# Two attention blocks on one core: a weight's sums and the weight loads behind the softmax sums' trips, a variance product one step earlier, the last block in two halves

## The chip, the core and the metric

The kernel runs on one core of one Trainium2 chip. The core has five engines that run side by side and meet through semaphores: TensorE (PE, the matrix products), VectorE (DVE), ScalarE (ACT), GpSimd (POOL), and SyncE (SP), which here issues nearly all DMA transfers. [...]The metric is device time in microseconds (us), the median of several executions; everything is float32.

## The reference, cut to what matters

Eight images of 512 channels by 1024 positions go through two attention blocks. Written for one image x (512 x 1024):

```
# block 0: 8 heads of 64 channels
h = group_norm(x, 32 groups);  q, k, v = Wqkv @ h + b
w = softmax(q_head^T k_head / sqrt(64));  a_head = v_head w^T
x = x + Wp @ a + bp
# block 1: one head of 512 channels
h = group_norm(x, 8 groups);  q, k, v = Wq @ h, Wk @ h, Wv @ h   (+ biases)
w = softmax(q^T k / sqrt(512))
x = x + Wp @ (v w^T) + bp
```

## The kernel before

**Products of weights.** Block 1 is rewritten: q^T k becomes h^T (Wq^T Wk) h and Wp Wv becomes one matrix. So the prologue computes two 512 x 512 products of weights, called m and z (`product`, L838). Each is copied out of PSUM by ACT (L848), stored to DRAM (L850), and loaded again in quarters (`prepare`, L279).

**Strassen's scheme in Winograd's form.** Nearly every large product is made of seven products of quarters instead of eight. `wino` (L229) does one such product: `step(p)` runs product p for two row blocks i, in three pairs of PSUM banks a, b and c, and `done` is called when an output quarter (row, column) is complete; u2 (the tile u) and u3 (the tile w) are partial results that DVE adds up at products 6 and 7 (`upper`, L240). The last two products, 4 and 3, are put on a list (`tail`) and run inside the next stage, by `finish`. Hooks are functions called after each step, and `background` is a list from which every step takes a few functions more (`back`). The factors need sums of quarters: four additions or subtractions of 128 x 512 on DVE for a weight (`left_sums`, called in `prepare`, L289 and L290). For the two-level form of the products (`conv2`), `keep2` (L300) makes four more on DVE or POOL, and SP stores seven pieces (L316). `keep` (L294) stores the one-level factors of a weight, 1.8 MB (L295); `load_weight` (L327) loads the factors of the next use, 1.3 or 1.8 MB (L335, L338).

**The prologue** (L871) handles the first image and all weights: transposes of Wk and Wq, the product m with the group norm's two small products inside it as hooks (`group_mean` after product 6, `affine` after product 9, counting from 0), then v (`by_token`), q and k of image 0, then the product z. `affine` (L121) is a small PE product over the groups, then one DVE instruction, four on POOL (L126 to L132), and then the scaling of the four tiles of the image, two on POOL and two on ACT. The background in v's stage holds the eight sums for the image's factors, and then the four sums for q and the four for k.

**Attention of block 0** (`attention0`, L639). The loop runs over four pairs of heads (hp) and two halves of the positions (tb). For each, PE makes eight score tiles (sc), ACT takes the exponential of each (e, L658), DVE adds the eight up (L660 and six times L662), and PE multiplies them with v (av). After tb = 1 the sums of the pair go on a trip (`reciprocals`, L593): PE adds over the partitions (sums), DVE copies the result out of PSUM (L617), SP stores it (L619) and loads it in another layout (L622), DVE takes reciprocals (L624), SP stores them (L625) and loads them twice as a broadcast (L635); a DVE or POOL multiplication then scales a (L696). The list `extra` has two slots for each (hp, tb): the even one is emptied between the scores and av, the odd one after av and before the trip. For image 0 these slots also hold what the prologue returns as `later`:

```
later = {
    1: steps, 2: [lambda: keep("z", t), load, load], 5: [load],
    12: [
```

Slot 1 is after the first av, slot 2 in the middle of the second block (hp 0, tb 1), slot 5 after av of hp 1, tb 0. `steps` are the four DVE sums for z, `load` a `load_weight`. What is pinned (`tc.keep_in_program_order`) keeps its place in the order of the program; what is not, may be moved on its engine by the scheduler.

**Attention of block 1** works on the image before the one in block 0; for the last image its `values1` (L790) is the end of the kernel. There a `wino` over the exponentials and z's factors makes the output quarters in the order of products 1, 2, 5, 6, 7, 4, 3. `done` adds the partial result u (L802), multiplies by the reciprocals r (L803), adds bias and residual (L805), and stores 128 x 512 numbers (L806). At the very end PE makes one 1 x 1 product (ps_good) for a flag that says whether all reciprocals were in range (L1213 to L1219), and every engine reads that flag (L1358) to decide on a slower general path, which isn't taken.

Of the kernel before, what the change touches and what calls it, by code (L numbers as in the profile page):

```python
# [12 lines left out]
ALU = mybir.AluOpType  # L13
AX = mybir.AxisListType

P = 128
# [13 lines left out]
def two_attention_blocks_kernel(  # L30
# [8 lines left out]
    nc = tc.nc  # L39
    B, C, T = x.shape  # L40
    KC = C // P
    HT = T // 2
# [16 lines left out]
    def matmul(*args, **kw):  # L59
        tc.keep_in_program_order(nc.tensor.matmul(*args, **kw))  # L60
# [113 lines left out]
    def main_path(ctx):  # L174
# [18 lines left out]
        def acc_tile(name):  # L193
            return ps_acc.tile([P, HT], F32, tag="acc", name=name)
# [14 lines left out]
        def load_x(b, c, what):  # L209
            t = big_tile(f"{what}_{b}_{c}")  # L210
            nc.sync.dma_start(t, x[b, c * P : (c + 1) * P, :])
            return t


        background = []
# [10 lines left out]
            while tail:  # L226
                tail.pop(0)()

        def wino(uid, mm, done, middle=(6, 2, 5, 7), hooks=(), after=(), back=2):  # L229

            hooks = list(hooks)
            ps, t1, u2, u3 = {}, {}, {}, {}
            bank = {1: "a", 2: "a", 6: "b", 7: "b", 4: "b", 5: "c", 3: "c"}

            def u_tile(what, i):
                return upool.tile([P, HT], F32, tag=f"{what}{i}", bufs=2 if what == "t" else 1, name=f"{what}{i}_{uid}")

            def upper(t, i, what):
                t[i] = u_tile(what, i)
                nc.vector.tensor_add(t[i], ps["b", i], t1[i])  # L240

            def step(p):
                n = bank[p]
                for i in range(2):
                    start = (n, i) not in ps
                    if start:
                        ps[n, i] = ps_pools["abc".index(n)].tile([P, HT], F32, tag="ps", name=f"ps{n}{i}_{uid}")
                    mm(p, i, ps[n, i], start)
                    if p == 1:
                        t1[i] = u_tile("t", i)  # L250
                        nc.scalar.copy(t1[i], ps["a", i])
                    elif p == 2:
                        done(i, 0, 0, ps["a", i], None)
                    elif p == 6:
                        upper(u2, i, "u")
                    elif p == 7:
                        upper(u3, i, "w")
                        done(i, 1, 1, ps["c", i], u3[i])
                    elif p == 4:
                        done(i, 1, 0, ps["b", i], t1[i])  # L260
                    elif p == 3:
                        done(i, 0, 1, ps["c", i], u2[i])
                run_background(back)
                for f in hooks.pop(0) if hooks else ():
                    f()

            step(1)
            finish()
            for p in middle:
                step(p)  # L270
            tail.extend([lambda: step(4), lambda: step(3), *after])


# [18 lines left out]
            return t, steps  # L292

        def keep(n, t):  # L294
            nc.sync.dma_start(wdram[n], t)  # L295


        wdram2 = {n: dram.tile([P, 7, 7, P], F32, name=f"sums2_{n}") for n in "qkmvp"}
# [489 lines left out]
            return total, {p: [x[:, i, :] for x in fs[p] for i in range(2)] for p in fs}  # L788

        def values1(b, zf, ef, r, xt, uid, hooks):  # L790
            def mm(p, i, ps, start):
                for k in range(4):
                    matmul(
                        ps, zf[p][k // 2][:, k % 2, ts(i, P)], ef[p][k], start=start and k == 0, stop=k == 3, skip_group_check=True
                    )

            def done(i, row, c, ps, u):
                oc = 2 * row + i

                o = acc_tile(f"o_{uid}_{oc}_{c}") if (row, c) == (1, 1) else ps  # L800
                if u is not None:
                    nc.vector.tensor_add(o, ps, u)  # L802
                nc.vector.tensor_mul(o, o, r[:, c, :])  # L803
                xh = xt[oc][:, ts(c, HT)]
                nc.vector.scalar_tensor_tensor(xh, o, obias[1][:, oc : oc + 1], xh, ALU.add, ALU.add)  # L805
                nc.sync.dma_start(out[b, oc * P : (oc + 1) * P, ts(c, HT)], xh)  # L806

            wino(f"av_{uid}", mm, done, middle=(2, 5, 6, 7), hooks=hooks, back=4)


        def raw(n, i):
# [59 lines left out]
        def prologue():  # L871
# [13 lines left out]
            def normed():  # L885
# [2 lines left out]
                    norm.apply(nc.scalar if c % 2 else nc.gpsimd, h0[c], h0[c], c)  # L888

            product(  # L890
                wq, wk, "m", {6: lambda: norm.group_mean(acc_tile("gmean_0_0")[:, :KC]), 9: normed},
            )
            raw_v = raw("v", 6)
            raw_p = raw("p", 7)
            for f in first["v"][1]:
                f()
            background.extend(steps)
            for n in "qk":
                background.extend(first[n][1])
            v = by_token(weight_factors(first["v"][0]), hf, "v0_0", middle=(2, 5, 6, 7), back=4)  # L900
            finish()
            run_background(len(background))
            keep2("v", first["v"][0], nc.vector)
            x1 = [load_x(1, c, "x1") for c in range(KC)] if B > 1 else []
            norm1 = GroupNorm(0, "0_1")
            background.extend(lambda c=c: norm1.stats(c, x1[c]) for c in range(len(x1)))
# [3 lines left out]
            t, steps = prepare("m")  # L910
# [7 lines left out]
            for f in p0_steps:  # L918
# [6 lines left out]
            t, steps = prepare("z")  # L925
            load = lambda: load_weight(tc.keep_in_program_order)
            later = {
                1: steps, 2: [lambda: keep("z", t), load, load], 5: [load],
                12: [
                    lambda: tc.keep_in_program_order(nc.vector.tensor_copy(ubias, bias[0])),  # L930
                    lambda: tc.keep_in_program_order(nc.vector.tensor_add(obias[1], bias[1], pcols("bp1"))),
                    lambda: tc.keep_in_program_order(nc.vector.tensor_add(obias[0], bias[2], pcols("bp0"))),
# [470 lines left out]
```

## Time and profile before

| | |
|---|---|
| median of 3 executions | 2808.33 us (2806.8 to 2808.77) |
| profiled execution, its own time | 2808.09 us |
| its span, from the first to the last instruction | 2806.30 us |
| mean granted PE clock | 0.998 of full speed |
| busy: PE, DVE, POOL, ACT | 2786.6, 1981.4, 1265.5, 986.3 us |
| PE waiting for another engine or a load, all waits | 11.8 us |
| bytes moved by DMA | 320.10 MB, mean 114 GB/s |

In the lines of the profile, L60 is the helper through which every product of the main path goes, so PE's lines are told apart by the tile's name; a tile's name is that in the code without its number (ps + bank + stage for PSUM: psb_v is bank b in v's stage). A timeline line has the start and the duration in us, the engine, the line, the operation, what it writes and reads, its shape, how many instructions are merged, and in brackets how long the engine had been idle before it and what ended that. PE instructions overlap, so the pitch between starts counts and not the duration of one. A float32 product takes two PE instructions.

### The profile page before, as it was taken

What the parts mean: (1) busy time and instruction counts of PE and PEld (TensorE: products, weight loads), DVE (VectorE), ACT (ScalarE), POOL (GpSimd) and SP (SyncE); (2) the same over time, 40 slices, a digit from 0 to 9 for tenths busy, and PEclk for the clock granted to TensorE, in tenths of its full rate; (3) what the DMA queues carried; (4) which work ended last, traced back from release to release, by engine and by line L of the source; (5) the groups of instructions that cost most, each with busy time, mean ns of one, the idle gap of its engine ahead of it and who ended that gap; (6) DMA issues with size and microseconds to landing.
All of it is one profiled execution on the core that took longest, in us unless ns stands there. A gap on an engine that the chain in (4) does not pass through costs nothing.

```text
span 2806.3 us, 35081 instructions
## 1 busy us (share of the span) xinstructions
PE 2786.6 (99%) x12756; PEld 1749.4 (62%) x12756; DVE 1981.4 (71%) x3018; ACT 986.3 (35%) x1275; POOL 1265.5 (45%) x1300
## 2 busy tenths in 40 slices
PE   9999999999999999999999999999999999999999
PEld 5436736776376853768538594485844868348584
DVE  5477777667776777766776767766678756787665
ACT  1253354214632146312463125531255212633130
POOL 2302705745067440774308652185521846137572
PEclk9999999999999999999999999999999999999999
DMA  8744512234123441134401343114521035112301
GB/s 285 226 161 139 196 32 70 111 146 178 34 67 131 152 153 39 62 139 165 148 24 62 150 174 127 32 54 161 187 102 49 37 151 207 63 55 94 120 5 73
DMA packets 118525, 320.10 MB, mean 114 GB/s; under 512 B 19591, under 2 KB 57927, under 8 KB 107722
## 3 DMA queue, kind: packets, MB, share of 16 engines
q1 hardware_dynamic: 117758, 317.36, 31.7%
q8 instruction: 103, 1.69, 0.2%
q14 instruction: 76, 0.62, 0.1%
q10 hardware_dynamic: 588, 0.42, 0.0%
HBM read 247.13 MB, written 70.62 MB: 113 GB/s over the span
## 4 chain that ended last, share of the span: by engine, by line
PE 97%; DVE 2%; issue 1%; POOL 1%; DMA 0%; ACT 0%; SPq 0%; DVEq 0%; POOLq 0%
PE sc L60 16%; PE av L60 15%; PE psb_av L60 6%; PE psb L60 5%; PE psa_av L60 4%; PE psc_av L60 4%; PE psc L60 3%; PE psa L60 3%; PE psb_z L60 3%; PE psb_g L60 3%; PE psb_k L60 3%; PE psb_q L60 3%; PE psb_v L60 3%; PE psb_p L60 2%; PE psa_z L60 2%; PE psc_z L60 2%
## 5 line engine op out<-in xcount | busy, mean ns | idle before, releaser
L658 ACT ACTIVATE e<-sc 128x1024 f32<-128x1024 f32 x512 | 476.2, 1051 | 79.7 <-PE sc L60 79.7
L662 DVE TENSOR_TENSOR sum<-sum,e 128x1024 f32<-128x1024 f32 x384 | 470.5, 1225 | 35.8 <-ACT x L138 0.5
L60 PE MATMUL sc<-q,k 64*128 64x512 f32 x2048 | 458.4, 597 | 0.0
L60 PE MATMUL av<-e,v 128*64 128x512 f32 x2048 | 453.4, 595 | 0.0
L60 PEld LDWEIGHTS sc<-q,k 64*128 64x128 f32 x2048 | 190.7, 186 | 247.3 <-ACT e L658 120.3
L60 PEld LDWEIGHTS av<-e,v 128*64 128x64 f32 x2048 | 141.4, 137 | 299.0 <-issue 289.0
L421 POOL TENSOR_TENSOR inner_h<-x 128x256 f32<-128x256 f32 x16 | 14.8, 924 | 415.8 <-DVE x L1105 415.8
L660 DVE TENSOR_TENSOR sum<-e,e 128x1024 f32<-128x1024 f32 x64 | 79.2, 1237 | 103.7 <-ACT e L658 103.7
L681 ACT COPY a<-av 128x512 f32<-128x512 f32 x64 | 37.6, 587 | 319.4 <-PE av L60 308.1
L126 POOL TENSOR_TENSOR rstd<-ve,mhalf 128x4 f32<-128x4 f32 x16 | 16.7, 1043 | 263.9 <-DVE ve L124 263.9
L60 PE MATMUL psb<-inner,inner_h 128*128 128x256 f32 x448 | 115.6, 380 | 0.0
L60 PE MATMUL psa_av<-e,z 128*128 128x512 f32 x256 | 113.3, 595 | 0.0
L421 POOL TENSOR_TENSOR inner_h<-h 128x256 f32<-128x256 f32 x30 | 24.1, 805 | 186.9 <-DVE h L1105 119.8
L743 POOL TENSOR_TENSOR sum<-sum,e 128x1024 f32<-128x1024 f32 x32 | 81.4, 2543 | 28.9 <-ACT e L739 27.7
L60 PEld LDWEIGHTS psb<-inner,inner_h 128*128 128x128 f32 x448 | 84.5, 190 | 13.6 <-POOL inner L436 1.8
L469 ACT COPY psb_v<-psa_v 128x512 f32<-128x512 f32 (+1 forms) x28 | 14.5, 517 | 218.9 <-DVE x L805 155.1
L60 PE MATMUL psb_g<-inner_h,w_m 128*128 128x256 f32 x336 | 86.5, 385 | 0.3
L729 DVE TENSOR_TENSOR e<-psc,u 128x512 f32<-128x512 f32 x56 | 38.7, 691 | 65.5 <-PE psc L60 65.3
L542 POOL TENSOR_TENSOR v<-v,v 128x256 f32<-128x256 f32 x28 | 20.1, 727 | 143.5 <-DVE u_v L537 143.4
L60 PEld LDWEIGHTS psa_av<-e,z 128*128 128x128 f32 x256 | 48.0, 190 | 57.3 <-issue 56.6
L421 POOL TENSOR_TENSOR inner_h<-t_h 128x256 f32<-128x256 f32 x62 | 73.3, 1187 | 21.3 <-PE psc_av L60 16.1
L739 ACT ACTIVATE e<-e 128x1024 f32<-128x1024 f32 x64 | 65.3, 1053 | 46.7 <-DVE e L729 25.6
(433 smaller groups left out, 6088.6 us busy)
## 6 DMA issues: line engine op xcount, KB each, us to landing
r<-all_rows SPq DMA_DIRECT2D x78, 256.0 KB
x<-in_x SPq DMA_DIRECT2D x36, 512.0 KB
h<-in_x SPq DMA_DIRECT2D x32, 512.0 KB
spill<-x SPq DMA_DIRECT2D x32, 512.0 KB
x<-spill SPq DMA_DIRECT2D x32, 512.0 KB
out<-x SPq DMA_DIRECT2D x64, 256.0 KB
kept<-a SPq DMA_DIRECT2D x28, 512.0 KB
again<-kept SPq DMA_DIRECT2D x28, 512.0 KB
```

What stands on the lines that cost most here:

```text
L60: tc.keep_in_program_order(nc.tensor.matmul(*args, **kw))
L126: nc.gpsimd.tensor_tensor(rstd, ve, mhalf, ALU.pow)
L421: pin(engine.tensor_tensor(dst, x, y, ALU.subtract))
L469: nc.scalar.copy(ps["b"], ps["a"])
L542: nc.gpsimd.tensor_tensor(d, x, y, ALU.add)
L658: nc.scalar.activation(e, sc, AF.Exp, scale=(C // 8) ** -0.5)
L660: nc.vector.tensor_add(total, es[0], e)
L662: nc.vector.tensor_add(total, total, e)
L681: nc.scalar.copy(dst, av)
L729: nc.vector.tensor_add(dst[0], ps, x[0])
L739: nc.scalar.activation(e[c, cc, r], e[c, cc, r], AF.Exp, scale=scale)
L743: on = lambda dst, x, y: lambda: tc.keep_in_program_order(nc.gpsimd.tensor_tensor(dst, x, y, ALU.add))
```

## The change

There are four edits.

1. In `later`, z's four sums go from slot 1 to slot 3, z's store and the first load from slot 2 to slot 4 (the store is now pinned), the second load from slot 2 to slot 8, and the third from slot 5 to slot 12.
2. In the prologue, `normed` (with `affine`) is the hook of product 8 instead of 9.
3. k's four sums leave the background of v's stage; they are put into the background for q's stage, ahead of the next image's statistics.
4. In `values1`, for the last image only: a new hook `early` scales u2 by r and adds it with the bias to the residual, before product 4's `done`; the output (row 0, column 1) is then only multiplied by r and added. Its last row block (product 3, i = 1) is computed in two halves of 256 columns, each multiplied, added and stored by itself.

```diff
-        def wino(uid, mm, done, middle=(6, 2, 5, 7), hooks=(), after=(), back=2):
+        def wino(uid, mm, done, middle=(6, 2, 5, 7), hooks=(), after=(), back=2, early=None):
...
                     elif p == 4:
+                        if early:
+                            early(i, u2[i])
                         done(i, 1, 0, ps["b", i], t1[i])
...
         def keep(n, t):
-            nc.sync.dma_start(wdram[n], t)
+            return nc.sync.dma_start(wdram[n], t)
...
         def values1(b, zf, ef, r, xt, uid, hooks):
+            last = b == B - 1
+
             def mm(p, i, ps, start):
-                for k in range(4):
-                    matmul(
-                        ps, zf[p][k // 2][:, k % 2, ts(i, P)], ef[p][k], start=start and k == 0, stop=k == 3, skip_group_check=True
-                    )
+                cut = 2 if last and (p, i) == (3, 1) else 1
+                for part in range(cut):
+                    cols = ts(part, HT // cut)
+                    for k in range(4):
+                        matmul(
+                            ps[:, cols], zf[p][k // 2][:, k % 2, ts(i, P)], ef[p][k][:, cols],
+                            start=start and k == 0, stop=k == 3, skip_group_check=True,
+                        )
+
+            def added(xh, o, oc):
+                nc.vector.scalar_tensor_tensor(xh, o, obias[1][:, oc : oc + 1], xh, ALU.add, ALU.add)
+
+            def early(i, u):
+                xh = xt[i][:, ts(1, HT)]
+                nc.vector.tensor_mul(u, u, r[:, 1, :])
+                added(xh, u, i)
 
             def done(i, row, c, ps, u):
                 oc = 2 * row + i
+                xh = xt[oc][:, ts(c, HT)]
+                dst = out[b, oc * P : (oc + 1) * P, ts(c, HT)]
+                if last and (row, c) == (0, 1):
+                    cut = 2 if i == 1 else 1
+                    for part in range(cut):
+                        cols = ts(part, HT // cut)
+                        nc.vector.tensor_mul(ps[:, cols], ps[:, cols], r[:, c, cols])
+                        nc.vector.tensor_add(xh[:, cols], ps[:, cols], xh[:, cols])
+                        nc.sync.dma_start(dst[:, cols], xh[:, cols])
+                    return
...
-                xh = xt[oc][:, ts(c, HT)]
-                nc.vector.scalar_tensor_tensor(xh, o, obias[1][:, oc : oc + 1], xh, ALU.add, ALU.add)
-                nc.sync.dma_start(out[b, oc * P : (oc + 1) * P, ts(c, HT)], xh)
-
-            wino(f"av_{uid}", mm, done, middle=(2, 5, 6, 7), hooks=hooks, back=4)
+                added(xh, o, oc)
+                nc.sync.dma_start(dst, xh)
+
+            wino(f"av_{uid}", mm, done, middle=(2, 5, 6, 7), hooks=hooks, back=4, early=early if last else None)
...
             product(
-                wq, wk, "m", {6: lambda: norm.group_mean(acc_tile("gmean_0_0")[:, :KC]), 9: normed},
+                wq, wk, "m", {6: lambda: norm.group_mean(acc_tile("gmean_0_0")[:, :KC]), 8: normed},
             )
...
             background.extend(steps)
-            for n in "qk":
-                background.extend(first[n][1])
+            background.extend(first["q"][1])
...
             keep2("v", first["v"][0], nc.vector)
+            background.extend(first["k"][1])
...
             later = {
-                1: steps, 2: [lambda: keep("z", t), load, load], 5: [load],
-                12: [
+                3: steps, 4: [lambda: tc.keep_in_program_order(keep("z", t)), load], 8: [load], 12: [
+                    load,
```

In the changed kernel as built, the order on DVE is: the seven sums of (hp 0, tb 1), the four sums of z, the copy of the pair's sums (L617 before). At the end it is: the multiplication of the first half, the flag, its addition, the multiplication of the second half, its addition. On SP the store of the first half stands before the reading of the flag, and that of the second half after it. Elsewhere the order is the same as before.

## The prediction

> **What bounds the kernel now.** I read the page first, for the busy shares. TensorE (PE) has matmuls in flight for all but 20 us of the span, so the change can only pay where PE stands still or runs slowly, or after its last product.
>
> ```profile
> PE 2786.6 (99%) x12756; PEld 1749.4 (62%) x12756; DVE 1981.4 (71%) x3018; ACT 986.3 (35%) x1275; POOL 1265.5 (45%) x1300
> ```
>
> Second, PE's waits (total us, times, longest). There are nine in all; these three lie where the change works. The 3.6 us for the first load, and five of 0.2 to 0.5 us, are not touched.
>
> ```profile
> PE sums L60 <- DVE sum L662: 5.1, 1, 5.1
> PE psa_v L60 <- POOL h L140: 0.8, 1, 0.8
> PE psb_v L60 <- DVE w_v L240: 0.5, 1, 0.5
> ```
>
> Third, PE's timeline over the first two head pairs (start us, us, what).
>
> ```profile
> 147.48 0.64 PE L60 MATMUL sums<-sum,ones 128*32 128x256 f32 x8
> 153.17 1.08 PE L60 MATMUL sums<-sum,ones 128*32 128x256 f32 x8 [5.06 <-DVE sum L662]
> 154.18 8.70 PE L60 MATMUL sc<-q,k 64*128 64x512 f32 x32
> 162.82 7.09 PE L60 MATMUL av<-e,v 128*64 128x512 f32 x32
> ...
> 183.92 1.07 PE L60 MATMUL sums<-sum,ones 128*32 128x256 f32 x16
> 184.92 7.14 PE L60 MATMUL sc<-q,k 64*128 64x512 f32 x32
> 191.99 7.09 PE L60 MATMUL av<-e,v 128*64 128x512 f32 x32
> ```
>
> The same piece (16 sums, 32 scores) takes 191.99 - 183.92 = 8.07 us at the second head pair and 162.82 - 147.48 = 15.34 us at the first: 7.27 lost, not 5.06. The stretches say why: fields are PE, PEld, DVE, ACT, POOL busy, then PE's clock.
>
> ```profile
> 153.10:154.20 1.10, 1.03 (x10) 0.22 (x10) 0.02 (x1) 0.00 (x0) 0.00 (x0) 0.50 0.97 417
> 154.20:156.00 1.80, 1.80 (x8) 0.83 (x6) 0.69 (x1) 0.00 (x0) 0.00 (x0) 0.50 0.97 410
> ```
>
> After standing still, PE ran at half clock. Fourth, who made it wait: VectorE (DVE).
>
> ```profile
> 123.84 7.87 DVE L662 TENSOR_TENSOR sum<-sum,e 128x1024 f32<-128x1024 f32 x6
> 141.38 0.69 DVE L289 TENSOR_TENSOR prepare_z<-prepare_z 128x512 f32<-128x512 f32 x1 [9.67 <-DMA prepare_z<-product_z]
> ...
> 143.93 1.22 DVE L660 TENSOR_TENSOR sum<-e,e 128x1024 f32<-128x1024 f32 x1
> 145.25 7.87 DVE L662 TENSOR_TENSOR sum<-sum,e 128x1024 f32<-128x1024 f32 x6
> ```
>
> DVE stood 9.67 us on the load of z, with the second block's softmax sums queued behind it; they ended at 153.1, while PE asked at 148.0.
>
> **What the Trainium skill says here.** (1) "TensorE: Matmul & The Clock Gate", What's actually happening: about 3.4 us of idling halves PE's clock, and about 3.4 us of work restores it. The trace agrees: 5.06 us idle, then 0.50 until about 157.4. (2) The same page's table of specifications calls VectorE's queue strictly first in, first out. The trace agrees: the exponentials that the sums need were made from 134.57 on, and the sums began at 143.93. (3) "PSUM — Partial Sum Buffer", PSUM bank collisions raise a hardware error: two engines must be kept off one bank even on different columns. No trace here shows a collision; but in the changed kernel as built, DVE's first half-block multiply waits for the count of the last of the block's eight product pairs, so the halves don't overlap with PE. (4) "DMA: Bandwidth & Descriptors", Anatomy of one DMA: about 2 us of fixed cost. The trace's small trips agree: the reload of the sums is issued 1.75 us after their store (187.53 and 185.78).
>
> **The change, part by part.**
>
> *z sums from slot 1 to slot 3.* The four DVE instructions (141.38 to 144.00, 2.6 us) now stand behind the second block's seven sums. Those can start at 136.5: ACT's chain starts at 134.57 with 0.93 a tile, and the first sum needs two tiles. They last 153.12 - 143.93 = 9.19, so they end at 145.7, 1.8 us before PE's av ends at 147.48. PE's wait goes, and the half clock with it: gain 7.27, between 7.0 and 7.4. Newly late is the copy of the sums out of PSUM (L617): behind the z steps it runs from 148.4, against PE's sums ready at 148.55. Nothing is added. If the z load lands later than 145.7 instead of 141.4, DVE stalls again, but PE next asks it for sums at about 178, and DVE has 31 us for 23 us of work there: 8 us of cover.
>
> *z's store and the weight loads.* Each is about 1.8 MB at most. They leave SP's queue ahead of the first trip of the sums (store, reload, reciprocals, broadcast) and go behind the trips of pairs 0, 1 and 2, so the queue entries after them are the storing of a and the next trip, 20 us on. At the 410 GB/s of the stretch above, 3.6 MB take 9 us. v's first weights are needed at 242.3, k's at 264.5; they are issued at about 160 and 217. Cost nothing; without that cover, each us of lateness is one of PE's.
>
> *Variance product one step earlier.* A product is two PE instructions of 0.43 us: 0.86. The deviations it needs were ready at 17.84 and it ran at 19.57, so 18.71 makes no new wait. Behind it hang the chain on POOL, two scalings on ACT, and ACT's copies of the weight product.
>
> ```profile
> 25.25 1.04 ACT L848 COPY prodm<-ps_wm 128x512 f32<-128x512 f32 x2
> 25.91 7.14 PE L60 MATMUL psa_v<-prepare_v,h 128*128 128x256 f32 x32 [0.81 <-POOL h L140]
> ```
>
> The page blames h on POOL, but the first h was ready at 24.24; the first copy, which frees the bank, ends at about 25.8. Both move by 0.86, PE's products would allow 24.9, so it starts at 25.05: gain 0.86 (0.5 to 1.0).
>
> *k's sums out of the v stage.* At 40.68 four of them (2.6 us) stood before the two w_v. PE's two steps from 39.80 to 47.51 took 7.71 against 2 x 3.46 for its neighbours: 0.79 lost, all regained (0.5 to 0.8); w_v then starts when its product ends. The four go into q's stage, where DVE idled 4.23 us for the next image; they finish near 60 and k needs them at 78. Their first delays u_q by about 0.4 us, with 6 us of room. Three stores of k move on SP from 43.3 (0.8 us each) to behind q's four, which end at 69.5; SP then waited for POOL until 75.58, so they fit. But two of the last four now stand behind POOL's last operation: about 1.1 us later for the load of m. It landed by 90.7 and DVE asked at 93.75; PE arrives 1.7 earlier. Margin 1.9 less at most 1.1. Cost nothing, up to 3 if that cover is gone.
>
> *The tail.* Matmuls: 16 of 0.216 us instead of 8 of 0.43, no difference. The u scalings (2 x 1.4 us) fall into DVE gaps of 2.74 and 2.67 us ahead of the w steps: no cost. At the end:
>
> ```profile
> 2799.39 0.70 DVE L802 TENSOR_TENSOR psc_av<-psc_av,u_av 128x512 f32<-128x512 f32 x1 [1.21 <-PE psc_av L60]
> 2800.00 0.14 DVE L1219 TENSOR_SCALAR flag<-ps_good 1x1 int32<-1x1 f32 x1
> 2800.12 0.70 DVE L803 TENSOR_TENSOR psc_av<-psc_av,r 128x512 f32<-128x512 f32 x1
> 2800.86 0.75 DVE L805 SCALAR_TENSOR_TENSOR x<-psc_av,obias,x 128x512 f32<-128x512 f32 x1
> ```
> ```profile
> L1358 SPq TENSOR_LOAD <-flag x1: 486/486/486, 2800.2 to 2800.2; - x1
> ```
>
> Now 2.22 us from 2799.39. After: four 128x256 operations (0.42 each by the rows of L537) one after another, with the flag in the first gap: 4 x 0.45 = 1.8. But SP issues the first half's store at 0.91, then loads the flag (0.75 us with the two instructions after it), and only then the second half: 0.91 + 0.33 + 0.75 = 2.0 against 2.25 now. Gain 0.25, plus about 0.2 for half the bytes (256 KB moved in some 0.75 us; shorter rows, so not the full 0.37): 0.45. Bounds: -0.1 if the shorter operations cost 0.5; 1.2 if the halves overlapped after all.
>
> **Sum.** 7.27 + 0.86 + 0.79 + 0.45 = 9.37 us. The profiled execution took 2808.09, of which 1.79 lie around its span of 2806.30; the span becomes 2796.9, that execution 2798.7. The median shown is 0.24 above it: 2799.0.
>
> **The rivals.**
> - *The clock does not come back*: the half-clock stretch stays, as after any gap. For it: the clock is a window in time, not a wait. Against: at the same place in pair 2 there is no gap and the clock is 1.00. It gives 2799.0 + 2.2 = 2801.2.
> - *A new wait in the prologue or no gain in the tail*: the load of m comes later than DVE's in-order need, or parts of the 0.86 and 0.79 are taken by another operand. For it: margins of 1 to 2 us. It costs 1 to 3 us: 2800.0 to 2802.0, at worst about 2803.
> - *Slower*: z's load lands so late that DVE, in order, holds the first trip and then pair 1's sums. It would have to land after 154 (12.6 us later than now) to cost PE anything, and after about 163 to eat all 9.4 us; each further us is one on the end, some 2811 with a second half-clock stretch. For it: the queue of the DMA engines is full there (share about 1). Against: with the weight loads gone the queue is shorter.
>
> **How the numbers follow.** The sum as worked: 0.80; the clock 0.05; prologue or tail 0.11; slower 0.04. The parts' bounds give 2797.4 to 2800.5, and medians of three here spread by 2 us; with the first rival inside, 2797.0 to 2801.7. A measurement of this kernel tells about 0.2% (5.6 us) from no change: faster means under 2802.7. That takes the sum, the clock and most of the third: 0.91; same 0.05; slower 0.04.
>
> **What would show it.** PE's wait for sums is gone and the stretch at 148 to 157 has clock 1.00; 16 sums and 32 scores take 8.1 us there; prepare_z on DVE stands after the seventh sum, without a wait. psa_v starts near 25.05, psb_v's third step without a gap. The last store is issued 1.9 to 2.1 us after the last product. Wrong would be a wait of over 1 us at sums, tr_wv or psa_k, or a first half-block operation that begins before PE's last product.

## The result, and the profile after

The changed kernel takes 2798.68 us (median of 8 runs, 2798.54 to 2799.47) against 2807.71 us before (8 runs, 2806.8 to 2809.11): ratio 0.9967, 95% interval 0.9957 to 0.9977. The forecast was 2799.0. The profiled execution took 2799.0 us and its span is 2797.1 us, 9.2 less than before.

The page's first line now has PE busy for all but 12.7 us of the span:

```profile
PE 2784.4 (100%) x12764; PEld 1752.8 (63%) x12764; DVE 1989.0 (71%) x3022; ACT 985.4 (35%) x1275; POOL 1267.3 (45%) x1300
```

PE's waits (total us, times, longest). These are all that are left of nine:

```profile
PE tr_wk L63 <- DMA rawk<-in_w: 3.8, 1, 3.8
PE tr_wv L63 <- DVE k L399: 0.5, 1, 0.5
PE ps_wm L60 <- DVE natq L860: 0.5, 1, 0.5
PE psc_v L60 <- DVE c_v L539: 0.2, 1, 0.2
```

Gone are the three waits that the prediction aimed at (sums, psa_v, psb_v), but also psc_p (0.4 us) and tr_wq (0.2 us, a wait for a load), which it had counted among the waits that are not touched. PE's timeline at the first head pair:

```profile
146.15 1.07 PE L60 MATMUL sums<-sum,ones 128*32 128x256 f32 x16
147.15 7.14 PE L60 MATMUL sc<-q,k 64*128 64x512 f32 x32
154.22 7.09 PE L60 MATMUL av<-e,v 128*64 128x512 f32 x32
```

The 16 sums and 32 scores take 154.22 - 146.15 = 8.07 us, to the hundredth what the second pair took before. The stretch behind the sums (busy of PE, PEld, DVE, ACT, POOL, then the clock) has the full clock:

```profile
147.00:150.00 3.00, 3.00 (x19) 1.43 (x16) 0.69 (x1) 1.61 (x2) 0.00 (x0) 1.00 0.01 3
```

On DVE z's sums stand behind the seventh softmax sum, with no wait for the load of z, which had cost 9.67 us:

```profile
136.54 7.88 DVE L664 TENSOR_TENSOR sum<-sum,e 128x1024 f32<-128x1024 f32 x6
144.33 0.68 DVE L291 TENSOR_TENSOR prepare_z<-prepare_z 128x512 f32<-128x512 f32 x1
145.05 1.90 DVE L292 TENSOR_TENSOR prepare_z<-prepare_z 128x512 f32<-128x512 f32 x3
147.29 0.69 DVE L619 COPY line<-sums 128x512 f32<-128x512 f32 x1 [0.34 <-PE sums L60]
```

In v's stage PE's third step follows the second at the pitch of its neighbours, 3.45 us, where it took 4.15 (first line before, the others after):

```profile
43.95 3.72 PE L60 MATMUL psb_v<-prepare_v,t_h 128*128 128x256 f32 x16 [0.53 <-DVE w_v L240]
39.27 3.62 PE L60 MATMUL psb_v<-prepare_v,h 128*128 128x256 f32 x16
42.72 3.62 PE L60 MATMUL psb_v<-prepare_v,t_h 128*128 128x256 f32 x16
46.18 3.62 PE L60 MATMUL psc_v<-prepare_v,h 128*128 128x256 f32 x16
```

At the end, DVE does the last block in two halves, with the flag between them, and SP reads the flag between the two stores (first lines DVE; then SP's own, whose columns are durations, count by time of start):

```profile
2790.32 0.43 DVE L821 TENSOR_TENSOR psc_av<-psc_av,r 128x256 f32<-128x256 f32 x1 [2.03 <-PE psc_av L60]
2790.66 0.14 DVE L1244 TENSOR_SCALAR flag<-ps_good 1x1 int32<-1x1 f32 x1
2790.78 0.42 DVE L822 TENSOR_TENSOR x<-psc_av,x 128x256 f32<-128x256 f32 x1
2791.24 0.43 DVE L821 TENSOR_TENSOR psc_av<-psc_av,r 128x256 f32<-128x256 f32 x1
2791.71 0.42 DVE L822 TENSOR_TENSOR x<-psc_av,x 128x256 f32<-128x256 f32 x1
```
```profile
L1383 SPq TENSOR_LOAD <-flag x1: 519/519/519, 2791.6 to 2791.6; - x1
L1383 SPq FUSED_REGOPS  x1: 187/187/187, 2792.2 to 2792.2; - x1
```
```profile
2792.58 0.34 SPq L823 DMA_DIRECT2D out<-x  x1
```

**Where the time came from.** Cutting both spans at the starts of the same PE instructions gives the table (us). The stretch between psa_q and the first sums, 96.52 us in both, is left out. The table closes on the 9.18 by which the spans differ.

| stretch of PE | before | after | gained | predicted |
|---|---|---|---|---|
| start to gmean (first loads) | 16.70 | 17.03 | -0.33 | 0 |
| gmean to psa_v (variance product) | 9.21 | 8.35 | 0.86 | 0.86 |
| psa_v to psa_q (k's sums) | 25.05 | 24.25 | 0.80 | 0.79 |
| first sums to the next av (z's sums) | 15.34 | 8.07 | 7.27 | 7.27 |
| that av to the last block | 2629.50 | 2629.01 | 0.49 | 0 |
| last block to the end of the span | 13.98 | 13.89 | 0.09 | 0.45 |

Three terms are exact to 0.01, the tail is a fifth of its size, and two entries were not in the sum at all: they cancel in part. The first of these is no effect of the change: in the thirteen traces of this document the stretch up to gmean takes 16.40 to 19.22 us, with the same instructions in it. The right total is therefore no proof of every step, and the experiments go after the last two rows and after the mechanism of the 7.27.

### The profile page after: what moved, and what is told of

Read it like the earlier page. It is cut to its first block, busy times and chain, and to the rows that moved or that the text cites. A ratio compares the mean times of both kernels' runs of the same rounds, so it can differ in the third digit from the quotient of the medians.

```text
span 2797.1 us, 35099 instructions
## 1 busy us (share of the span) xinstructions
PE 2784.4 (100%) x12764; PEld 1752.8 (63%) x12764; DVE 1989.0 (71%) x3022; ACT 985.4 (35%) x1275; POOL 1267.3 (45%) x1300
## 4 chain that ended last, share of the span: by engine, by line
PE 98%; DVE 1%; POOL 0%; DMA 0%; issue 0%; POOLq 0%
PE sc L60 16%; PE av L60 16%; PE psb_av L60 6%; PE psb L60 5%; PE psa_av L60 4%; PE psc_av L60 4%; PE psc L60 3%; PE psa L60 3%; PE psb_z L60 3%; PE psb_v L60 3%; PE psb_g L60 3%; PE psb_k L60 3%; PE psb_q L60 3%; PE psb_p L60 2%; PE psa_z L60 2%; PE psc_z L60 2%
## 5 line engine op out<-in xcount | busy, mean ns | idle before, releaser
L736 POOL TENSOR_TENSOR e<-e,e 128x512 f32<-128x512 f32 x64 | 79.4, 1270 | 2.0 <-DVE e L731 1.9
```

The lines of the kernel that those rows point to most:

```text
L736: nc.gpsimd.tensor_tensor(blocks(dst, r, cc)[0], blocks(x, r, cc)[0], blocks(y, r, cc)[0], ALU.add)
```

## The experiments

Each run is given by its median, its range and number of runs, and its ratio to the runs of the kernel before on the same chip.

**One edit at a time.** Kernels with edit 1 alone, with edits 2 and 3 alone, with edit 4 alone, and the changed kernel without the halves. The edit of the first, from the kernel before (apart from `keep`, which returns its instruction, it is all of it):

```diff
-                1: steps, 2: [lambda: keep("z", t), load, load], 5: [load],
-                12: [
+                3: steps, 4: [lambda: tc.keep_in_program_order(keep("z", t)), load], 8: [load], 12: [
+                    load,
```

> Only the first edit: z's sums in slot 3, z's store and the loads in slots 4, 8 and 12. My theory (the wait cost its own 5.06 us and another 2.2 us of half clock): 16 sums and 32 scores of the first pair take 8.1 us instead of 15.34, PE's clock there is 1.00, and the median falls by 7.3 us to 2800.4. Rival (the half clock is a window in time and stays): the stretch takes 10.2 us and the median is 2802.6. Rival (the wait moves to the next trip): a PE wait of over 1 us at a later sums, and a median over 2803.

Measured 2799.88 us (2799.73 to 2800.72, 7 runs), ratio 0.9970 (0.9959 to 0.9981). First sums to the next av: 8.07 us. Edit 1 alone gives the whole 7.27 at this place; the clock needs nothing else to stay up. The middle stretch came down too, to 2628.70.

The second (from the kernel before):

```diff
-"gmean_0_0")[:, :KC]), 9: normed},
+"gmean_0_0")[:, :KC]), 8: normed},
...
-            for n in "qk":
-                background.extend(first[n][1])
+            background.extend(first["q"][1])
...
             keep2("v", first["v"][0], nc.vector)
+            background.extend(first["k"][1])
```

> Only the second and third edits: the variance product after product 8, and k's four sums in q's stage. My theory: psa_v starts 0.86 us earlier against the mean's product, the five steps of v lose no 0.8 us, the median falls by 1.66 to 2806.0, and PE's waits at psa_v and psb_v are gone while that of 5.1 us at sums stays. Rival (POOL's scaling of h, which the page names, ends later than ACT's copies, or w_v is held by something else): one of the two stays at 0.3 us or more, and the median is 2806.6 to 2807.3.

Measured 2806.72 us (2804.86 to 2807.13, 13 runs), ratio 0.9993 (0.9985 to 1.0001). The trace has the 0.86 and the 0.80, the same as in the changed kernel, and no wait at psa_v and psb_v. (Which of the two ended the old wait at psa_v stays open: in every trace psa_v starts 0.1 us behind the end of ACT's first copy, and also with the end of POOL's second h, and both moved with the edit.) The median lies where the rival had it, but not for the rival's reason: 0.35 is given back at the first sums, where the piece now takes 15.69 us, although the wait itself is shorter:

```profile
PE sums L60 <- DVE sum L662: 4.4, 1, 4.4
```

That a shorter wait costs more is taken up in the part on the clock. The third has only the diff of `values1` and `wino` in "The change":

> Only the fourth edit: u scaled ahead, the last block in two halves. My theory after the result (one bank serializes the halves, and SP reads the flag between the two stores): from the start of the last product pair to the last store's issue 9.3 us as before, the median falls by 0.1 to 2807.6. The step as I predicted it (SP's flag reading costs no more than 0.75 us): minus 0.45, 2807.25. Rival (the halves overlap with PE): the last store is issued 1.0 us earlier and the median is 2806.5.

Measured 2808.47 us (2806.84 to 2810.04, 13 runs), ratio 1.0000 (0.9992 to 1.0009). In its trace the last store is issued 9.34 us behind the start of the last block's products (before: 9.31), and the span ends 13.87 us behind it (before: 13.98). So the trace has 0.11 us at the tail, too little for these medians to show, and neither the 0.45 of the prediction nor the rival's 1.0 is there. The fourth (from the changed kernel):

```diff
-                cut = 2 if last and (p, i) == (3, 1) else 1
+                cut = 1
...
-                    cut = 2 if i == 1 else 1
+                    cut = 1
```

> The changed kernel with the last block whole again: u is still scaled ahead, but the last row block is one product of 512 columns, one multiplication, one addition, one store. My theory (only the early scaling pays, the halves cost): after the last product 0.70 + 0.73 us on DVE, the flag is read by SP meanwhile, the last store is issued 1.6 us after the last product instead of 2.27, its transfer is 0.2 longer: 0.4 to 0.5 us better than the changed kernel, 2798.2. Rival (the halves pay, as the change means them to): 0.3 us or more slower than the changed kernel, 2799.0.

Measured 2798.99 us (2798.38 to 2799.38, 5 runs), ratio 0.9965 (0.9952 to 0.9979). The expected half was right: with one whole block SP has done with the flag before the data are ready, and the store is issued 8.76 us behind the start of the block, 0.6 sooner than with the halves. The conclusion was wrong: the span ends 14.15 us behind it, not sooner but 0.26 later (after: 13.89), about as the rival had it. So the last store's issue, by which both the prediction and this theory had reckoned, does not set the end alone.

**What sets the end of the span.** Behind the flag each engine takes a branch around the general path. After:

```profile
L1384 PEldq COMPARE_BRANCH  x1: 3735/3735/3735, 2791.4 to 2791.4; - x1
L1384 PEldq EVENT_SEMAPHORE  x1: 51/51/51, 2795.2 to 2795.2; - x1
L1384 DVEq EVENT_SEMAPHORE  x1: 21/21/21, 2795.4 to 2795.4; - x1
L1384 SPq EVENT_SEMAPHORE  x8: 17/17/17, 2795.2 to 2795.7; - x8
```

PE's branch takes 3.7 us, and PE's and DVE's next instructions stand 3.8 and 2.9 us behind the starts of their branches (DVE's is at 2792.6). In the kernel without halves PE's branch took 4.33 us and PE's and SP's last instructions stood at 2796.1, later than after. That gave the theory for three more runs. The first keeps the right half of the last block in a PSUM bank of its own, so that the left half can be finished beside PE:

```diff
+            right = []
...
-                cut = 2 if last and (p, i) == (3, 1) else 1
+                cut = 2 if last and i == 1 and p in (5, 3) else 1
+                if cut == 2 and not right:
+                    right.append(acc_tile("right_half"))
                 for part in range(cut):
+                    ps = right[0] if part else ps
...
```

Left out are the lines in `done`, which read the right half from that bank, and do so for the quarter (row 1, column 1) of product 5 too, whose addition of u is split in two.

> The changed kernel, but the right half of the last image's last block has a PSUM bank of its own from product 5 on, so that the left half's two DVE operations can run while PE still multiplies the right half, and both stores are issued ahead of SP's read of the flag. The last store's issue should come some 1.2 us sooner than after's 9.35 us behind the start of the last block's products. Theory: the end of the span is not set by that store but by the engines' leaving the branch that follows the flag (PE's branch took 3.5 to 4.3 us in six traces, and SP's last wait ends with it or with DVE's, 1.4 us ahead of the span's end in each). PE's branch moves by nothing here, so at most the 0.3 us between PE's leaving and SP's last wait are won: 13.6 to 13.9 us from the start of the last block to the end of the span (13.87 after), time about 2798.5. Rival, the last store's issue sets the end: 12.7 us, time about 2797.4.

Measured 2798.39 us (2798.3 to 2798.66, 5 runs), ratio 0.9964 (0.9951 to 0.9978). The left half is now multiplied 1.7 us ahead of the right one, beside PE:

```profile
2789.03 0.43 DVE L826 TENSOR_TENSOR psc_av<-psc_av,r 128x256 f32<-128x256 f32 x1 [0.30 <-PE psc_av L60]
2790.76 0.43 DVE L826 TENSOR_TENSOR right_half<-right_half,r 128x256 f32<-128x256 f32 x1 [0.84 <-PE right_half L60]
```

The last store is issued at 8.01 us instead of 9.35. The span ends at 13.01: 0.88 won, between the theory's 0.3 and the rival's 1.2. Neither is right as written. In the changed kernel it was SP that ended last; once its store is early, SP is done first, and PE's leaving is the next:

```profile
L1393 SPq EVENT_SEMAPHORE  x8: 17/17/17, 2793.9 to 2794.4; - x8
L1393 PEldq COMPARE_BRANCH  x1: 3752/3752/3752, 2791.9 to 2791.9; - x1
L1393 PEldq EVENT_SEMAPHORE  x1: 51/51/51, 2795.7 to 2795.7; - x1
```

The second leaves the block as it was, and puts the judgement ahead of the last two products:

```diff
         layer1_rest(B - 1, inner, gf, gsteps, [], [[]] * 4, ())
-        finish()
-
         assert len(taken) == stretches
...
         nc.vector.tensor_scalar(flag, ps[0:1, 0:1], -1.0, float(P), ALU.mult, ALU.add)
+        finish()
```

> The changed kernel, but the judgement on the reciprocals (ps_good and flag) stands ahead of the last image's last two products instead of behind them: the engines find the flag ready when they reach its read. Theory (leaving the branch sets the end): PE branches 0.8 to 0.9 us sooner, DVE only by the 0.14 us of the flag's operation, since it reads the flag behind its last operation; the later of the two sets the end, so 0.1 to 0.3 us are won: 13.6 to 13.8 us from the start of the last block to the end of the span, time about 2798.5. Rival (last store's issue sets the end): SP's read of the flag goes ahead of the stores and the last store is issued some 0.6 us sooner: 13.25 us, time about 2798.1.

Measured 2799.0 us (2798.44 to 2801.13, 5 runs), ratio 0.9966 (0.9952 to 0.9979). 13.52 us: 0.37 won, where the theory had 0.1 to 0.3 and the rival 0.6. PE was out of the branch 5 us before DVE, which reads the flag behind its last operation and now ends last, 1.0 us ahead of the span's end:

```profile
L1382 PEldq EVENT_SEMAPHORE  x1: 51/51/51, 2793.0 to 2793.0; - x1
L1382 SPq EVENT_SEMAPHORE  x8: 17/17/17, 2796.6 to 2797.2; - x8
L1382 DVEq EVENT_SEMAPHORE  x1: 21/21/21, 2798.3 to 2798.3; - x1
```

The third has both edits:

> The last two edits together on the changed kernel. Theory (leaving the branch sets the end): now PE branches 0.8 us sooner and DVE, whose last operation ends 0.4 to 0.8 us sooner, too: 12.9 to 13.2 us from the start of the last block to the end of the span, time about 2797.8. Rival (the last store's issue sets the end): no more than the separate bank alone gives, 12.7 us there and here, time about 2797.4. If neither holds, all three of these runs stand at 13.9 us.

Measured 2802.85 us (2801.62 to 2804.48, 15 runs), ratio 0.9981 (0.9973 to 0.9989). The end came as the new reading wants it, 12.29 us, but the kernel lost 5 us ahead of it: ps_good needs a PSUM bank, the right half holds one of the two, and PE stood at ps_good until DVE gave the other one back. That was my oversight, and no theory had it.

```profile
2779.56 0.19 PE L60 MATMUL ps_good<-ones,both 128*1 128x1 f32 x2 [3.24 <-DVE x L810]
```

The fourth has the own bank as above, and makes the judgement a hook behind product 5, when a bank is free (the body of `judge` is the moved text):

```diff
-        layer1_rest(B - 1, inner, gf, gsteps, [], [[]] * 4, ())
-        finish()
+        def judge():
...
+        layer1_rest(B - 1, inner, gf, gsteps, [], [[]] * 4, [[], [], [judge]])
+        finish()
```

> The right half's own bank and the early judgement together once more, but with ps_good behind product 5, when a bank is free, and not in front of product 4, where it waited 3.2 us for one. Expected from the four ends seen so far (the end of the span stood 1.0 us behind the later of PE's and DVE's leaving the branch, or 1.4 us behind SP's last wait, whichever was last): no wait of PE at ps_good, 12.2 to 12.6 us from the start of the last block to the end of the span as in the run with the wait, against 13.03 with the bank alone and 13.87 after; time 0.5 to 0.8 us under the bank alone, about 2797.7. If the end is set by the last store's issue alone, as much as with the bank alone: 13.0 us, 2798.4.

Measured 2797.89 us (2797.13 to 2799.75, 5 runs), ratio 0.9966 (0.9952 to 0.9979). No wait at ps_good, 12.37 us to the end, span 2795.3. The eight ends side by side, all in us behind the start of the last block's products, with the time at which the last store has landed. The times are those of the traces' own records; the views print spans to 0.1 us, so the expectations have 13.87 and 13.03 for 13.89 and 13.01.

| kernel | last store issued | it has landed | PE leaves | DVE leaves | SP's last wait | end of span |
|---|---|---|---|---|---|---|
| before | 9.31 | 12.58 | 12.30 | 12.61 | 12.60 | 13.98 |
| after | 9.35 | 11.95 | 12.00 | 12.21 | 12.51 | 13.89 |
| edit 4 alone | 9.34 | 11.93 | 11.81 | 12.22 | 12.49 | 13.87 |
| no halves | 8.76 | 12.75 | 12.85 | 11.66 | 12.77 | 14.15 |
| own bank | 8.01 | 10.17 | 12.01 | 11.46 | 10.73 | 13.01 |
| flag sooner | 8.93 | 10.77 | 7.15 | 12.50 | 11.33 | 13.52 |
| both, with the wait | 8.01 | 10.35 | 7.13 | 11.18 | 10.91 | 12.29 |
| both, without it | 8.01 | 10.43 | 7.16 | 11.15 | 10.99 | 12.37 |

One rule fits all eight rows within 0.03: the end is the latest of PE's leaving + 1.0, DVE's leaving + 1.0 and SP's last wait + 1.4. The offsets were read from rows ahead of the last; for the last row the rule was written down before the run, and it held. The five other traces of this document, from which no offset was read, fit within 0.02; in all five SP's last wait decides.

The traces also show what SP waits for there. It steps through eight semaphores, about 0.08 us each, and one of them is raised when the last store has landed. Before, that is the eighth; after, it is the first, and SP then still has the other seven to step through, from 11.96 to 12.51:

```profile
L1359 SPq EVENT_SEMAPHORE  x8: 17/17/17, 2802.6 to 2804.9; - x8
```

So the smaller second store of the changed kernel did land sooner, 2.60 us behind its issue and not 3.27, and the seven further steps took most of that back. The whole last block without halves was issued sooner and took 3.99 us to land; by the rule, that is why this kernel ended later.

The length of PE's branch goes with a transfer of another kind. In all thirteen traces a packet of 16 KB, on a queue that the profile calls instruction, starts 1.0 to 1.4 us behind the start of PE's branch, and PE leaves 1.5 to 1.7 us behind that packet's end. The packet takes 0.9 to 1.2 us, but 1.8 in the kernel without halves, where the last store moves at the same time and the branch is longest. After (packets, MB, share of the engines' time):

```profile
q8 instruction: 2, 0.03, 0.7%
```

It looks as if PE had to load the instructions behind the branch; no run varied that. The last kernel's trace is 1.8 us shorter than the changed kernel's, of which 1.5 lie at the end and 0.6 in the first loads, where executions differ anyway. Its median is 0.8 lower, the ranges overlap, and the ratios to the kernel before are alike (0.9966 and 0.9967): that it is faster as a whole than the changed kernel is not shown.

**Which half of edit 1 works, the sums or the loads?** The changed kernel with the weight loads back in their old slots:

```diff
-                3: steps, 4: [lambda: tc.keep_in_program_order(keep("z", t)), load], 8: [load], 12: [
-                    load,
+                2: [load, load], 3: steps, 4: [lambda: tc.keep_in_program_order(keep("z", t))], 5: [load],
+                12: [
```

> The changed kernel with z's weight loads back at the points of the order where they stood before, ahead of the first trips, and only z's sums and the keeping behind them. Theory: the sums on DVE alone made PE wait, the loads on SP only lengthened the first trip, which is hidden: no wait of PE at sums, 8.1 us from the first sums to the next av as after, the first trip's load lands 1 to 2 us later, time 2798.7. Rival, the loads' place is what counts: PE waits 3 us or more at sums or at the products behind the trips and the time goes to 2802 or more. Beside that: if the small stalls of 0.2 to 0.3 us near 482, 1387 and 2040 us, which the kernels without this edit have and those with it have not, come from the loads' place, they are back here, 0.5 to 0.8 us.

Measured 2800.12 us (2799.63 to 2800.34, 6 runs), ratio 0.9970 (0.9958 to 0.9982). PE doesn't wait at sums and the piece takes 8.07 us: the sums alone give the 7.27, and the rival is out. The trip's reload of the sums is issued 5.7 us behind their store instead of 1.8 (153.98 and 148.31; after, 149.81 and 148.01), more than the 1 to 2 us later that I had expected, and no PE wait follows. But the median is 1.4 us above the changed kernel's (about half of that may be the chip's: the kernel before took 0.75 us more there), and its trace says where it lost: against after it falls back by 0.23 us near 475, 0.27 near 1378, 0.30 near 2031 and 0.11 near 2491 (times of the trace after). The wait that had gone is back:

```profile
PE psc_p L60 <- DVE c_p L539: 0.4, 1, 0.4
```

The first three steps are in all four traces with the loads in the old slots (before, edits 2 and 3 alone, edit 4 alone, and this one) with the same sizes, 0.8 us together, and in none of the nine others. So the loads' place is worth about 0.8 us by the traces, in images whose instructions are in the same order in both kernels. How an order 300 to 1900 us earlier reaches them is open.

**The clock: how much of a wait is lost?** Dummy operations on DVE ahead of the first pair's row totals in the changed kernel bring the wait back at will; they add work whose result nobody uses.

```diff
+            wait6 = const.tile([P, 6], F32, name="wait6")
...
+                1: [lambda: [tc.keep_in_program_order(nc.vector.bn_stats(wait6, q[0][:, :HT])) for _ in range(16)]],
                 3: steps, 4: [lambda: tc.keep_in_program_order(keep("z", t)), load], 8: [load], 12: [
```

> The changed kernel with 16 dummy operations on DVE (statistics of 128x512, some 0.61 us each, their result unused) ahead of the row totals of image 0's first pair, so that PE has to wait at sums again, by some 16 x 0.615 - 7.15 = 2.7 us. Theory (the wait's cost is its length and, from a certain length on, a clock halved for a stretch of some 3.4 us or twice that, of which PE works the part behind the wait): at 2.7 us the clock holds and the loss is 2.7 us, time about 2801.4; if the clock still falls, 4.4 us, about 2803. Rival (the half clock has nothing to do with this wait): 2.7 us here and only the wait's length in the next run too.

> The same with 20 dummy operations: PE waits some 20 x 0.615 - 7.15 = 5.15 us at sums, about as long as in the kernel before, but with z's sums and loads where the change puts them. Theory: the clock is halved behind the wait as it was before (1.7 to 2.2 us on top), 12.9 to 15.4 us from the first sums to the next av's start, loss 6.9 to 7.4 us, time about 2805.8. Rival (the half clock came from something else in the old order, DMA traffic or the order itself): 13.2 us, loss 5.15 us, time about 2803.8.

Measured with 16: 2805.75 us (2804.47 to 2806.67, 12 runs), ratio 0.9992 (0.9984 to 1.0001); with 20: 2806.18 us (2805.05 to 2807.12, 12 runs), ratio 0.9994 (0.9986 to 1.0003). With 20 the wait was 5.23 us and the piece 15.51 long, 7.44 lost: within 0.1 of the upper ends of the theory's ranges, and the rival's 13.2 is out. With 16 I had the wait too short (3.64 and not 2.7), and then the loss was far above both expectations: 6.41 of it at this piece.

```profile
150.36 1.08 PE L60 MATMUL sums<-sum,ones 128*32 128x256 f32 x8 [3.64 <-DVE sum L664]
```
```profile
148.00:149.00 1.00, 0.00 (x0) 0.00 (x0) 0.98 (x1) 0.00 (x0) 0.00 (x0) 0.92 0.00 0
149.00:150.00 1.00, 0.00 (x0) 0.00 (x0) 0.92 (x1) 0.00 (x0) 0.00 (x0) 0.50 0.00 0
...
155.00:156.00 1.00, 1.00 (x6) 0.48 (x4) 0.00 (x0) 0.80 (x1) 0.00 (x0) 0.66 0.00 0
156.00:157.00 1.00, 1.00 (x6) 0.38 (x4) 0.74 (x1) 0.85 (x2) 0.00 (x0) 1.00 0.08 8
```

The clock column is the stretch's mean: 0.92 means half clock from 148.84 on, 0.66 until 155.68. Read so in six kernels, with the loss taken from the pieces' lengths (for ps_good's wait, from the run without it):

| kernel | PE waits (us) | half clock, length | of it at work | wait + half of that | measured loss | PE busy in the 3.41 us before it | in its first 3.41 us |
|---|---|---|---|---|---|---|---|
| ps_good's wait | 3.24 | 3.41 | 3.41 | 4.95 | 5.00 | 32% | 100% |
| 16 operations | 3.64 | 6.83 | 5.31 | 6.30 | 6.41 | 38% | 56% |
| edits 2 and 3 alone | 4.42 | 6.83 | 6.18 | 7.51 | 7.62 | 0% | 81% |
| edit 4 alone | 4.64 | 6.83 | 5.61 | 7.45 | 7.55 | 0% | 65% |
| before | 5.06 | 6.83 | 4.21 | 7.17 | 7.27 | 29% | 23% |
| 20 operations | 5.23 | 6.83 | 4.20 | 7.33 | 7.44 | 24% | 23% |

Wait and half of the work in the stretch give every loss within 0.11 us. The stretch is 3.41 us long or twice that, and starts 2.1 to 4.3 us behind PE's last product, in no order with the length of the wait. Both fit a clock that is set anew every 3.41 us by how busy PE was: the Trainium skill, "TensorE: Matmul & The Clock Gate", What's actually happening, states such a window (3413 ns) and that it runs free of the kernel.

The traces agree. The clock falls once more behind PE's last product. In the five kernels with a wait at sums that fall comes 2652.15 to 2652.16 us after the first one, though from the start of the wait to the end of PE's work it is 2650.5 to 2651.8 us; with ps_good's wait it comes after 17.07 us. These are 777 and 5 windows of 3.4133 us. So the windows' edges can be counted back from the last fall in every trace.

How busy must PE be? The thirteen traces, cut into these windows, have 19 falls and 19 rises of the clock. PE was busy for 40% of the window or less ahead of each fall, and for 51% or more in each of the 10,592 windows behind which the full clock stayed. The two cases nearest to each other, edit 1 alone (51%, the clock holds for another window) and flag sooner (40%, it falls):

```profile
2789.67:2793.09 3.42, 1.73 (x6) 0.47 (x4) 2.17 (x5) 0.00 (x0) 0.00 (x0) 1.00 0.20 77
2793.09:2796.50 3.41, 0.00 (x0) 0.00 (x0) 0.45 (x1) 0.00 (x0) 0.00 (x0) 1.00 0.27 91
```
```profile
2791.50:2794.91 3.41, 1.37 (x7) 0.86 (x5) 1.71 (x4) 0.00 (x0) 0.00 (x0) 1.00 0.28 105
2795.00:2796.00 1.00, 0.00 (x0) 0.00 (x0) 0.00 (x0) 0.00 (x0) 0.00 (x0) 0.50 0.43 149
```

Once halved, the clock came back behind windows that were busy for 86% or more, and not behind those of 81% or less, as the first half-clock window of edits 2 and 3 alone. The 86% is from the start of the kernel with its own bank (4.76 to 8.18): there the traces have no clock record yet, but the first one is a rise to full, and PE's transposes start 0.21 us apart ahead of it and 0.11 behind it. The shares are those of the records, whose ends are modelled, so the two limits, between 40 and 51% and between 81 and 86%, are estimates.

By these windows a wait costs up to 3.4 us beyond its length (half of two windows, if PE works through both), by where it falls in the window: edits 2 and 3 alone shortened it by 0.64 us and lost 0.35 more.

## Why the prediction was right, and where not

**The z wait.** Right to the hundredth, 7.27, because the two pieces were compared whole and not the idle time alone. The step "the second block's softmax sums queued behind it" held: moving the sums is all that it took (old load slots). The softmax sums ended 1.7 us ahead of PE's av (144.42 and 146.15; worked out: 1.8), and the loads, the trip and z's own load cost PE no wait, as it said. The first rival, the clock that doesn't come back, fell: without the wait the clock stays at 1.00, and with it back by dummy work it falls again.

**The variance product and k's sums.** 0.86 and 0.80 against 0.86 and 0.79. psa_v started at 25.38 and not 25.05, but this execution ran 0.33 later from its first loads, ahead of the change. The load of m, on which the second rival rested, made no wait: DVE takes it at 92.43 without a stop.

**The tail.** The step that failed is "SP issues the first half's store at 0.91, then loads the flag (0.75 us with the two instructions after it)... 2.0 against 2.25": the order was as said, but from the first store's end to the second's start (2791.58 to 2792.58) it took 1.0 us, not 0.75, so the last store came 2.26 behind the first operation and the 0.25 was not gained. The check in the prediction, 1.9 to 2.1 us, failed with 2.3. The other part, 0.2 for half the bytes, was too small: issue to landing is 0.67 us shorter. But the sum had no term for what follows the landing, and SP's seven further semaphores took some 0.55 back. Behind it lies a frame that was too narrow: the sum took the end for the last store's alone, and reckoned with its issue. The whole block (issued 0.6 us sooner, landed 0.8 later, ended 0.26 later) showed that the issue doesn't give the landing, and the own bank (issued 1.3 sooner, ended 0.88 sooner) that PE's branch sets the end once the store is early. The second rival's half "no gain in the tail" was the true case here.

**The middle.** "Cost nothing" for the weight loads was wrong in sign: their new place gives about 0.8 us in images 300 to 1900 us on. The table shows only 0.49, since the changed kernel has a 0.24 us stall near 2425 that the kernel before has not. That stall is in all eight traces with edits 2 and 3 and no dummy work, and in none of the five others; why is open. No step of the prediction looked beyond the first image.

**The total.** 9.37 predicted and 9.18 found in the traces (9.0 by the medians): the tail's missing 0.36 and the later start's 0.33 stand against the 0.49 of the middle. That the whole came within 0.2 is luck in these three entries; the 8.9 us of the other three terms is not.

## What to carry to other kernels

Price a wait of PE by comparing the whole piece with the same piece elsewhere: the idle time is only a part, and a shorter wait can cost more. Before the last transfer is made earlier, list for every engine when it is last held, the flag and the branch at the end among them, since the next latest takes over. When a move pays in full, check all other stretches too; here 0.5 us had come from where nobody had looked.

## What had not been expected of the hardware

- A wait of 3.24 us halved PE's clock, though in no window of 3.41 us was PE idle throughout (32% busy). The page named above speaks of a whole idle window; here 40% busy was too little and 51% enough, and the measurement decides. The part behind the wait cost 1.7 to 3.1 us (half of 3.41 to half of 6.18).
- PE's branch around the general path takes 3.5 to 4.3 us in the traces here and goes with a transfer on an instruction queue; DVE's next instruction comes 2.9 to 3.5 us behind its branch. With the flag early, PE's share lies beside its last products and DVE's work and costs nothing.
- SP's read of the flag and what follows it up to the next store took 1.0 us of SP's queue (2791.58 to 2792.58): a store queued behind such a read is late by that much.
- A store that lands sooner frees the end only as far as SP's order of waits lets it: with the last store's semaphore first of eight instead of last, 0.63 us of earlier landing left 0.09.
